# Where a transformer block sums its last softmax and its MLP's weight blocks

## The chip, the cores and the metric

The kernel runs on one core of a Trainium2 chip. The core has a matrix engine (TensorE, PE in the profile, with PEld for its weight loads), VectorE (DVE), ScalarE (ACT), GpSimd (POOL) and SyncE (SP), which issues most of the DMA transfers. Each engine works off its own queue in order and waits on semaphores for the others. TensorE reads SBUF and writes PSUM; the other engines take its results from there. The metric is the device time of one execution in microseconds (us), the median of several runs; lower is better.

## The reference, cut to what matters

A transformer block in fp32 on x of 16 x 224 x 512, with a context of 16 x 750 x 512 and 16 heads of 32: self-attention, cross-attention, and an MLP of hidden width 2048.

```python
x = x + gate_a[:, None] * attn_out            # self-attention, 224 keys
c_attn_w = softmax(einsum('bhqd,bhsd->bhqs', q_c, k_c) * scale, axis=-1)   # 750 keys
x = x + (c_attn_w @ v_c) @ W_cproj + b_cproj
x_norm2 = modulate(_ln(x), shift_m, scale_m)
h = gelu(x_norm2 @ W_mlp1 + b_mlp1)           # 512 -> 2048
x = x + gate_m[:, None] * (h @ W_mlp2 + b_mlp2)
```

## The kernel before

Every helper line is recorded in the profile as line 28 (the wrapper `Ordered` that keeps instructions in program order), so the profile is read by tile names. A product of two 4-byte operands shows as two records per matmul call.

**Cross-attention** runs over 64 units, a unit being one batch and a group of four heads. The 750 keys lie on partitions in six chunks of 125; three tiles `pt` of a unit hold two chunks each for four heads and 224 queries. The units are pipelined: while one unit's scores are made, the unit before it gets its maxima subtracted (`subtract`, VectorE) and its exponentials (`weights`, ScalarE), and the one before that is multiplied with the values (`values`, TensorE). `weights(h)` is called for the heads in two halves (h is 0 or 1). After each exponential GpSimd adds that tile's chunks onto `acc`: five additions of 125x448 for each half, ten for a unit. `values` then makes 24 matmuls of weights and values into a PSUM bank `o`, and `sums` four matmuls of ones and `acc`, which give the softmax denominators in the same bank. `finish` normalizes (`normalize`, VectorE: a reciprocal and a product) into `at`, which `project` multiplies with `wcproj`.

**The transition** (lines 1114 to 1145) runs after the last unit's maxima. TensorE's queue holds, in this order: the unit before the last (`prev.values`), the four plain products of MLP tile 0 (`mlp_plain`, into the four banks of `sc`) with the transposes of the two `subtract` calls between them, the last unit's `cur.values`, two products of MLP tile 1 (`ahead.begin`, banks `mm`), the two halves of the last projection (banks 0 and 1 of `tail`, tile name `sc`), and the other five products of tile 1 (`ahead.rest`). VectorE's queue holds `subtract`, `mlp_turned`, `mlp_sums(1)`, `cur.finish`, the addition in `begin`, the two `upd` of the projection, and the evictions of `rest`. The projection's x is finished on GpSimd and written to the DRAM tile `x_cross` by SP's queue; behind that write, in the same queue, are the loads of `w1_3` and of the four parts of `w2`, 1 MB each.

**The MLP** runs over 7 groups of 512 tokens (`GT`). Its products of 2 x 2 blocks use seven block products instead of eight: sums of blocks of both operands are made first (`combine` for the left one, `combine_right` for the right one; four operations each). For the first layer `mlp_sums(i)` makes the sums of weight tile i (i is 0 to 3, 512 of the 2048 columns): the tiles `ws` and a quarter of `w` itself; `mlp_turned` makes those of the tokens (`tt`, and a quarter of `mxt`). An operation of either has 128x512 elements. For the second layer `sums_2` makes those of `w2` in two rounds of four operations with 128x1024 elements, round 0 from `w2[0]` and `w2[2]`, round 1 from `w2[1]` and `w2[3]`.

`First(i)` is one weight tile for one group of tokens: `begin` makes products 1 and 2, `rest` products 6, 5, 7, 3 and 4 on the banks a, b and c, with an eviction between them (VectorE copies or adds; ScalarE copies and applies the gelu). Products 7 and 4 go on accumulating in bank a, so each waits until the bank's earlier content is read. In the first group (q = 0), tile 0 is plain, tile 1 is `ahead`, and then come `first(2)`, `mlp_sums(3)` on VectorE, `sums_2` on GpSimd, `first(3)`, and `mlp_sums(0)` on GpSimd (lines 1260 to 1264). `second(q, half)` is the second layer for half of a group's tokens: seven products of 16 records each, with operations on h by VectorE between them (`s1`, then `a21`, `a11`, `a12`), evictions into `upd`, and `close`, two GpSimd operations and the output's store. `between(p)` is called at fixed places in it and puts there the next group's loads, norms, transposes (`mlp_turn`) and `mlp_turned`.

Of the kernel before, what the change touches and what calls it, by code (L numbers as in the profile page):

```python
# [10 lines left out]
AF = mybir.ActivationFunctionType  # L11
ALU = mybir.AluOpType
# [25 lines left out]
def kernel(  # L38
# [23 lines left out]
    nc = Ordered(tc)  # L62
    B, N, H = x.shape
# [10 lines left out]
    CP = 125  # L74
# [12 lines left out]
    GC = GT // P  # L87
    HT = GT // 2
    NW = MLP // H
# [69 lines left out]
    def load_w(pool, w, name, bufs=1):  # L159
        kc = w.shape[0] // P  # L160
        t = pool.tile([P, kc, w.shape[1]], F32, name=name, bufs=bufs)
        nc.sync.dma_start(out=t, in_=w.rearrange("(k p) n -> p k n", p=P))
        return t
# [91 lines left out]
    for i in range(2):  # L255
        lo = (2 + 3 * i) * H
# [106 lines left out]
    def sums(o, pts, rows):  # L363

        for i, pt in enumerate(pts):
            for s in range(HG):
                mm(
                    o[s * HD : (s + 1) * HD, N : 2 * N], ones[:rows, :HD], pt[:, s, :],
                    start=False, stop=(i == len(pts) - 1), skip_group_check=True,
                )  # L370
# [36 lines left out]
    first = {}  # L407
# [28 lines left out]
    if True:  # L436
# [190 lines left out]
        for i, (p, g, j) in enumerate(units):  # L627
# [6 lines left out]
            if was:  # L634
                pt = self_weights(*was, row)
# [20 lines left out]
        pt = self_weights(*was, row)  # L656
# [18 lines left out]
    mlp = {"w1": [], "ws": {}, "w2": [], "wt": [], "h": {}}  # L675
# [10 lines left out]
    def mlp_weights(pool, name):  # L686
        i = len(mlp["w1"])
        mlp["w1"].append(load_w(pool, w_mlp1[:, i * H : (i + 1) * H], name))

    def combine(engine, a11, a12, a21, a22, s1, s2, s3, s4):  # L690

        engine.tensor_tensor(s1, a21, a22, ALU.add)
        engine.tensor_tensor(s3, a11, a21, ALU.subtract)
        engine.tensor_tensor(s2, s1, a11, ALU.subtract)
        engine.tensor_tensor(s4, a12, s2, ALU.subtract)

    def combine_right(engine, b11, b12, b21, b22, t1, t2, t3, t4):

        engine.tensor_tensor(t1, b12, b11, ALU.subtract)
        engine.tensor_tensor(t3, b22, b12, ALU.subtract)  # L700
        engine.tensor_tensor(t2, b22, t1, ALU.subtract)
        engine.tensor_tensor(t4, b21, t2, ALU.subtract)

    def mlp_sums(engine, pool, i):

        w = mlp["w1"][i]
        mlp["ws"][i] = ws = pool.tile([P, 3, 2, HT], F32, name=f"ws{i}", bufs=1)
        lo, hi = w[:, :2], w[:, 2:]
        combine(
            engine, lo[:, :, :HT], hi[:, :, :HT], lo[:, :, HT:], hi[:, :, HT:],  # L710
            ws[:, 0], ws[:, 1], lo[:, :, HT:], ws[:, 2],
        )

# [5 lines left out]
    def mlp_norm(i):  # L719
        Norm([mx[i]], [mx[i]], P).all()  # L720
# [18 lines left out]
                )  # L739
            lo = to  # L740

    def mlp_turned(engine):

        mlp["tt"] = tt = mlp["in"].tile([P, 3, 2, HT], F32, name="tt")
        lo, hi = mlp["xt"][:, :2], mlp["xt"][:, 2:]
        combine_right(
            engine, lo[:, :, :HT], lo[:, :, HT:], hi[:, :, :HT], hi[:, :, HT:],
            tt[:, 0], tt[:, 1], lo[:, :, HT:], tt[:, 2],
        )

    def mlp_plain(ps, m):

        w, lo = mlp["w1"][m // KC], (m % KC) * P
        for k in range(KC):
            mm(ps[:, :GT], w[:, k, lo : lo + P], mlp["xt"][:, k, :], start=(k == 0), stop=(k == KC - 1))
# [4 lines left out]
    class First:  # L760
# [39 lines left out]
            self.product(c, 2, True)  # L800
            nc.vector.tensor_tensor(self.p1, c, self.p1, ALU.add)

        def rest(self, b):
            a = self.a
            self.product(a, 6, False)
            u2 = self.part()
            nc.vector.tensor_copy(u2, a)
            self.product(b, 5, True)
            p5 = self.part()
            nc.scalar.copy(p5, b)  # L810
            self.out(self.p1, 0, 0)
            self.product(a, 7, False)
            nc.vector.tensor_tensor(p5, a, p5, ALU.add)
            self.out(p5, 1, 1)
            self.product(b, 3, False)
            nc.vector.tensor_tensor(u2, b, u2, ALU.add)
            self.out(u2, 0, 1)
            self.product(a, 4, False)
            self.out(a, 1, 0)


    wqc, wcproj, wkc, wvc = cw["qc"], cw["proj"], cw["k"], cw["v"]
    cxt_pool = context_pools.enter_context(tc.tile_pool(name="cxt", bufs=3, side="right", reuse_waits="tile"))
    with tc.tile_pool(name="ca", bufs=2, reuse_waits="tile") as ca:
# [98 lines left out]
        for b in range(B):  # L923
            n = b + 1
            for g in range(KC):
                f, m = (b, g + 1) if g < KC - 1 else (n, 0)
# [50 lines left out]
        class Unit:  # L977
# [72 lines left out]
                    w4 = pt[:, 2 * h : 2 * h + 2, :].rearrange("p s (k t) -> p s k t", k=2)  # L1050
                    nc.vector.tensor_tensor(w4, w4, less.to_broadcast([CP, 2, 2, N]), ALU.add)

            def weights(self, h):

                if h == 0:
                    self.acc = ca.tile([CP, HG, N], F32, name="acc", bufs=2)
                acc = self.acc[:, 2 * h : 2 * h + 2, :]
                for n, pt in enumerate(self.pts):
                    w = pt[:, 2 * h : 2 * h + 2, :]
                    nc.scalar.activation(w, w, AF.Exp)  # L1060

                    if n == 0:
                        nc.gpsimd.tensor_tensor(acc, w[:, :, :N], w[:, :, N:], ALU.add)
                    else:
                        for j in range(2):
                            nc.gpsimd.tensor_tensor(acc, acc, w[:, :, j * N : (j + 1) * N], ALU.add)

            def values(self):
                b, g = self.b, self.g
                self.o = ps_o.tile([P, 512], F32, name="o")  # L1070
                for n in range(CH):
                    values(
                        self.o, self.pts[n], lambda s, kc: vt[b, kc][:, (g * HG + s) * HD : (g * HG + s + 1) * HD],
                        (2 * n, 2 * n + 1), CP, n == 0,
                    )
                sums(self.o, [self.acc], CP)

            def finish(self):
                t = ca.tile([P, N], F32, name="at", bufs=2 * KC)
# [14 lines left out]
        cur = prev = last = None  # L1094
        for b, g in units:
            cur, prev, last = Unit(b, g), cur, prev
# [20 lines left out]
        prev.finish()  # L1117
        mlp_plain(sc[:, 1], 1)
        cur.subtract(0)
        cur.weights(0)  # L1120
        mlp_plain(sc[:, 2], 2)
        cur.subtract(1)
        cur.weights(1)
        mlp_plain(sc[:, 3], 3)
        mlp_turned(nc.vector)
        mlp_sums(nc.vector, mlp["in"], 1)
        for m in range(KC):
            gelu(sc[:, m], mlp["h"][0][:, m], m)
        cur.values()
        cur.finish()  # L1130
        ahead = First(1)
        ahead.begin(*(ps_mm.tile([P, 512], F32, name="mm") for _ in range(2)))
        tail = ps_s.tile([P, HG, 512], F32, name="sc")
# [5 lines left out]
    with tc.tile_pool(name="ml", bufs=3, reuse_waits="tile") as ml:  # L1139
# [1 line left out]
            mlp["h"][i] = ml.tile([P, KC, GT], F32, name=f"h{i}", bufs=1)  # L1141
        mlp_weights(ml, "w1_3")
        ahead.rest(tail[:, 2])
        mlp_sums(nc.vector, ml, 2)
        attention_psum.close()

        mlp["w2"] = [load_w(ml, w_mlp2[i * H : (i + 1) * H, :], f"w2_{i}") for i in range(NW)]
        bmlp2 = bias_rows(ml, b_mlp2, P, "bmlp2")
        resid = {}

        def sums_2():

            for i in range(NW // 2):
                t12 = (
                    cw["pool"].tile([P, KC, H], F32, name="wcproj") if i == 0
                    else ml.tile([P, KC, H], F32, name="w2t12", bufs=1)
                )
                t4 = ml.tile([P, KC, HT], F32, name=f"w2t4_{i}", bufs=1)
                lo, hi = mlp["w2"][i], mlp["w2"][i + NW // 2]
                combine_right(  # L1160
                    nc.gpsimd, lo[:, :, :HT], lo[:, :, HT:], hi[:, :, :HT], hi[:, :, HT:],
                    t12[:, :, :HT], t12[:, :, HT:], lo[:, :, HT:], t4,
                )
                mlp["wt"].append((t12[:, :, :HT], t12[:, :, HT:], t4))

        def fetch(i):
            t = ml.tile([P, H], F32, name="xr")
# [4 lines left out]
        with (  # L1172
# [3 lines left out]
            def bank(name):  # L1176
                return ps_p.tile([P, 512], F32, name=name)

            def first(i):
                f = First(i)  # L1180
                f.begin(bank("a"), bank("c"))
                f.rest(bank("b"))

            def second(q, half, between):

# [69 lines left out]
            for q in range(NG):  # L1255
                if q:
                    for i in range(NW):
                        first(i)
                else:
                    first(2)  # L1260
                    mlp_sums(nc.vector, ml, 3)
                    sums_2()
                    first(3)
                    mlp_sums(nc.gpsimd, ml, 0)

                def between(half, p, i=(q + 1) * GC, more=q + 1 < NG):

                    if not more:
                        return
                    if (half, p) == (0, 1):  # L1270
                        for c in range(GC):
                            mlp_load(i + c)
                    for c, at in enumerate(((0, 6), (0, 5), (0, 7), (0, 3))):
                        if (half, p) == at:
                            mlp_norm(i + c)
                    for c, at in enumerate(((0, 7), (0, 3), (1, 2), (1, 5))):
                        if (half, p) == at:
                            mlp_turn(ps_mm, i + c)
                    if (half, p) == (1, 5):
                        mlp_turned(nc.vector)  # L1280

                for half in range(2):
                    second(q, half, lambda p, half=half: between(half, p))
# [36 lines left out]
```

## Time and profile before

| | us |
|---|---|
| median of 3 runs (lowest to highest) | 2915.72 (2912.17 to 2917.97) |
| profiled execution | 2912.48 |
| span of its trace, first to last instruction | 2910.7 |

The mean granted TensorE clock in the profiled execution is 0.993 of full speed. Cut into stretches, the trace gives:

| stretch, us from the span's start | what runs | TensorE busy | VectorE | ScalarE | GpSimd | granted clock |
|---|---|---|---|---|---|---|
| 0 to 630 | mostly self-attention | 614.4 | 418.4 | 131.8 | 122.4 | 1.00 |
| 630 to 2189 | rest of it, cross-attention | 1514.6 | 1198.6 | 853.5 | 955.5 | 0.99 |
| 2189 to 2315 | the transition, first MLP group | 115.2 | 76.3 | 23.3 | 58.7 | 0.96 |
| 2315 to 2910.7 | the other six groups | 589.6 | 236.5 | 111.0 | 105.2 | 1.00 |

All edited code belongs to the third stretch, in which TensorE stands still for 10.9 of 126 us; in the last one it does so for 6.1 of 595.7. A row of the timeline has the start, the time from its first instruction's start to its last one's end, the engine, the operation with output and inputs, partitions x elements, a count, and in brackets the engine's idle time before it and what ended that.

### The profile page before, as it was taken

The page shows a single profiled execution, that of the slowest core. Times are in us where ns is not written, and L with a number is a line of the kernel's source. Part 1 is how long each engine was busy: PE and PEld are TensorE (multiplying, and loading weights), DVE is VectorE, ACT ScalarE, POOL GpSimd, SP SyncE. Part 2 cuts the span into 40 slices and gives each one's busy share as a digit, 9 for nine tenths or more (in the row PEclk, how much of TensorE's full clock was granted, in tenths as well). Part 3 has the DMA queues.
Part 4 walks back from the last instruction along what each step waited for, and adds up shares of the span by engine and source line. Part 5 has one row for each costly group of instructions (what it writes and reads, how often), then busy time and mean ns, then how long its engine had stood idle before and what let it go on. Part 6 is the DMA issues. An engine that isn't in the chain of part 4 may idle for free.

```text
span 2910.7 us, 46976 instructions
## 1 busy us (share of the span) xinstructions
PE 2833.8 (97%) x19693; PEld 1809.3 (62%) x19693; DVE 1929.8 (66%) x2752; ACT 1119.6 (38%) x1402; POOL 1241.7 (43%) x1379
## 2 busy tenths in 40 slices
PE   8999999998999999999999999999978999999999
PEld 3444444444555565655655655666545888888888
DVE  4666776676478778787787787787785543444343
ACT  1222222221456655665565556656543112112211
POOL 1022222122357666676666666666654410221021
PEclk9999999999999999999999999999989999999999
DMA  6111110100100010100001100100013111110110
GB/s 191 59 33 33 32 33 10 60 11 29 52 32 24 22 35 24 35 32 21 29 25 34 35 24 23 34 25 24 22 44 107 55 37 37 44 57 29 46 44 29
DMA packets 55385, 114.44 MB, mean 39 GB/s; under 512 B 4309, under 2 KB 4373, under 8 KB 55173
## 3 DMA queue, kind: packets, MB, share of 16 engines
q1 hardware_dynamic: 54560, 110.58, 11.8%
q8 instruction: 155, 2.54, 0.4%
q10 hardware_dynamic: 612, 0.85, 0.1%
q14 instruction: 58, 0.47, 0.1%
HBM read 89.33 MB, written 22.09 MB: 38 GB/s over the span
## 4 chain that ended last, share of the span: by engine, by line
PE 79%; DVE 10%; ACT 5%; issue 4%; POOL 2%; DMA 1%; SPq 0%; POOLq 0%; ACTq 0%; DVEq 0%
PE mm L28 43%; PE a L28 10%; PE sc L28 10%; PE o L28 8%; PE b L28 5%; ACT pt L28 4%; DVE at L28 3%; PE c L28 3%; DVE top L28 2%; POOL acc L28 1%; DVE stats L28 1%; DVE m L28 1%; DVE mc L28 1%; ACT kt L28 1%; DMA gate<-gate_d 1%
## 5 line engine op out<-in xcount | busy, mean ns | idle before, releaser
L28 POOL TENSOR_TENSOR acc<-acc,pt 125x448 f32<-125x448 f32 x512 | 584.4, 1141 | 40.2
L28 ACT COPY pt<-sc 125x1792 f32<-125x1792 f32 x192 | 317.3, 1653 | 563.0 <-DVE top L28 509.9
L28 DVE TENSOR_TENSOR pt<-pt,o 125x896 f32<-125x896 f32 x384 | 394.2, 1081 | 87.0 <-PE o L28 84.6
L28 DVE TENSOR_TENSOR top<-top,sc 125x896 f32<-125x896 f32 x320 | 346.6, 1083 | 35.4 <-PE sc L28 28.7
L28 PE MATMUL mm<-wkvc,cxt 128*125 128x512 f32 x768 | 354.4, 604 | 6.9 <-ACT kt L28 6.9
L28 PE MATMUL mm<-cxt,wkvc 128*128 128x375 f32 x1024 | 353.3, 487 | 2.4 <-ACT cxt L28 2.4
L28 POOL TENSOR_TENSOR upd<-upd,gate 112x512 f32<-112x512 f32 (+1 forms) x60 | 78.9, 1315 | 631.7 <-DVE upd L28 627.1
L28 ACT ACTIVATE pt<-pt 125x896 f32<-125x896 f32 x384 | 338.3, 951 | 18.7 <-DVE pt L28 18.1
L28 POOL TENSOR_TENSOR acc<-pt 125x448 f32<-125x448 f32 x128 | 146.6, 1145 | 455.6 <-ACT pt L28 455.6
L28 PEld LDWEIGHTS mm<-cxt,wkvc 128*128 128x128 f32 x1024 | 184.7, 190 | 118.9 <-issue 15.4
L28 PEld LDWEIGHTS mm<-wkvc,cxt 128*125 128x125 f32 x768 | 136.4, 187 | 171.5 <-issue 153.3
L28 DVE RECIPROCAL at<-o 128x224 f32<-128x224 f32 x128 | 198.7, 1552 | 66.9 <-PE o L28 66.9
L28 ACT ACTIVATE pt<-sc 112x1792 f32<-112x1792 f32 x64 | 106.5, 1664 | 332.5 <-PE sc L28 327.9
L28 POOL TENSOR_TENSOR rstd<-mv,eps 112x2 f32<-112x2 f32 (+3 forms) x93 | 18.0, 193 | 468.7 <-DVE mv L28 468.7
L28 PE MATMUL sc<-qt,kt 32*125 32x224 f32 x3072 | 201.5, 376 | 13.9 <-ACT pt L28 13.3
L28 PE MATMUL mm<-xt,wqkv 128*128 128x448 f32 x512 | 208.6, 550 | 5.7 <-DVE xt L28 4.7
L28 DVE TENSOR_REDUCE m<-sc 112x8 f32<-112x1792 f32 x64 | 129.6, 2025 | 121.0 <-PE sc L28 121.0
L28 PEld LDWEIGHTS sc<-qt,kt 32*125 32x125 f32 x3072 | 132.9, 183 | 93.7 <-issue 33.4
L28 PE MATMUL o<-pt,vt 125*32 125x224 f32 x3072 | 158.6, 354 | 0.0
L28 PEld LDWEIGHTS mm<-xt,wqkv 128*128 128x128 f32 x512 | 92.0, 190 | 87.6 <-issue 80.4
L28 DVE TENSOR_REDUCE mc<-mm 112x8 f32<-112x512 f32 (+1 forms) x128 | 79.8, 666 | 98.4 <-PE mm L28 98.3
L28 ACT COPY mx<-a 128x512 f32<-128x512 f32 x26 | 15.2, 585 | 325.4 <-POOL upd L28 306.3
(187 smaller groups left out, 4687.2 us busy)
## 6 DMA issues: line engine op xcount, KB each, us to landing
cx<-in_ctx_dram SPq DMA_DIRECT2D x96, 250.0 KB
x<-in_x_dram SPq DMA_DIRECT2D x16, 448.0 KB
x_self<-x SPq DMA_DIRECT2D x16, 448.0 KB
x<-x_self SPq DMA_DIRECT2D x16, 448.0 KB
x_cross<-x SPq DMA_DIRECT2D x16, 448.0 KB
mx<-x_cross SPq DMA_DIRECT2D x28, 256.0 KB
w<-in_L_xcond_W_mlp_dram SPq DMA_DIRECT2D x7, 1024.0 KB
xr<-x_cross SPq DMA_DIRECT2D x28, 256.0 KB
```

Of the source, the lines that this page charges most:

```text
L28: return lambda *args, **kw: self.tc.keep_in_program_order(f(*args, **kw))
```

## The change

- **The last unit's softmax sums.** `weights` gets a switch `add`. For the last unit it is off: the exponentials are taken as before, the GpSimd additions are left out, and `values` gives `sums` the six chunks instead of `acc`: 24 matmuls of ones and weights in place of four.
- **Order in the transition.** `mlp_turned` and `mlp_sums(1)` stand behind `cur.finish()`.
- **Block sums as generators.** `combine` and `combine_right` yield after each operation, so that a caller can issue them one at a time; `every` issues what is left. All of them are on VectorE now.
- **Tile 2.** `rest` calls `between` after each of its five eviction steps. `first(2)` issues one operation of `mlp_sums(3)` at each.
- **Tile 3.** `first(3)` issues two operations of `sums_2` at each, which were on GpSimd ahead of it.
- **`mlp_sums(0)`**, which was on GpSimd behind `first(3)`, is issued on VectorE at the place `between(3)` of the first half of `second(0, ...)`.
- **Load order.** The four `w2` parts are loaded as 0, 2, 1, 3.

```diff
+    def every(steps):
+        for _ in steps:
+            pass
     def combine(engine, a11, a12, a21, a22, s1, s2, s3, s4):
-        engine.tensor_tensor(s1, a21, a22, ALU.add)
+        yield engine.tensor_tensor(s1, a21, a22, ALU.add)
...
-        def rest(self, b):
+        def rest(self, b, between=lambda: None):
             self.product(a, 6, False)
             nc.vector.tensor_copy(u2, a)
+            between()
             self.product(b, 5, True)
             nc.scalar.copy(p5, b)
             self.out(self.p1, 0, 0)
+            between()
             self.product(a, 7, False)
             nc.vector.tensor_tensor(p5, a, p5, ALU.add)
             self.out(p5, 1, 1)
+            between()
             self.product(b, 3, False)
             nc.vector.tensor_tensor(u2, b, u2, ALU.add)
             self.out(u2, 0, 1)
+            between()
             self.product(a, 4, False)
             self.out(a, 1, 0)
+            between()
...
-            def weights(self, h):
+            def weights(self, h, add=True):
+                if not add:
+                    for pt in self.pts:
+                        w = pt[:, 2 * h : 2 * h + 2, :]
+                        nc.scalar.activation(w, w, AF.Exp)
+                    self.acc = None
+                    return
...
-                sums(self.o, [self.acc], CP)
+                if self.acc is None:
+                    sums(self.o, [pt[:, :, j * N : (j + 1) * N] for pt in self.pts for j in range(2)], CP)
+                else:
+                    sums(self.o, [self.acc], CP)
...
-        cur.weights(0)
+        cur.weights(0, False)
...
-        cur.weights(1)
+        cur.weights(1, False)
         mlp_plain(sc[:, 3], 3)
-        mlp_turned(nc.vector)
-        mlp_sums(nc.vector, mlp["in"], 1)
         for m in range(KC):
             gelu(sc[:, m], mlp["h"][0][:, m], m)
         cur.values()
         cur.finish()
+        mlp_turned()
+        every(mlp_sums(mlp["in"], 1))
...
-        mlp["w2"] = [load_w(ml, w_mlp2[i * H : (i + 1) * H, :], f"w2_{i}") for i in range(NW)]
+        w2 = {i: load_w(ml, w_mlp2[i * H : (i + 1) * H, :], f"w2_{i}") for i in (0, 2, 1, 3)}
+        mlp["w2"] = [w2[i] for i in range(NW)]
...
-                combine_right(
-                    nc.gpsimd, lo[:, :, :HT], lo[:, :, HT:], hi[:, :, :HT], hi[:, :, HT:],
+                yield from combine_right(
+                    nc.vector, lo[:, :, :HT], lo[:, :, HT:], hi[:, :, :HT], hi[:, :, HT:],
...
-                    first(2)
-                    mlp_sums(nc.vector, ml, 3)
-                    sums_2()
-                    first(3)
-                    mlp_sums(nc.gpsimd, ml, 0)
+                    steps = mlp_sums(ml, 3)
+                    first(2, lambda: next(steps, None))
+                    every(steps)
+                    steps = sums_2()
+                    first(3, lambda: (next(steps, None), next(steps, None)))
+                    every(steps)
...
+                    if (i, half, p) == (GC, 0, 3):
+                        every(mlp_sums(ml, 0))
```

More of the change, by code (lines that the diff above doesn't have):

```diff
@@ L688, in mlp_weights, with mlp_sums @@
         mlp["w1"].append(load_w(pool, w_mlp1[:, i * H : (i + 1) * H], name))
+    def every(steps):
+        for _ in steps:
+            pass
     def combine(engine, a11, a12, a21, a22, s1, s2, s3, s4):
-        engine.tensor_tensor(s1, a21, a22, ALU.add)
-        engine.tensor_tensor(s3, a11, a21, ALU.subtract)
-        engine.tensor_tensor(s2, s1, a11, ALU.subtract)
-        engine.tensor_tensor(s4, a12, s2, ALU.subtract)
+        yield engine.tensor_tensor(s1, a21, a22, ALU.add)
+        yield engine.tensor_tensor(s3, a11, a21, ALU.subtract)
+        yield engine.tensor_tensor(s2, s1, a11, ALU.subtract)
+        yield engine.tensor_tensor(s4, a12, s2, ALU.subtract)
     def combine_right(engine, b11, b12, b21, b22, t1, t2, t3, t4):
[L699 to L704, printed above, removed]
+        yield engine.tensor_tensor(t1, b12, b11, ALU.subtract)
+        yield engine.tensor_tensor(t3, b22, b12, ALU.subtract)
+        yield engine.tensor_tensor(t2, b22, t1, ALU.subtract)
+        yield engine.tensor_tensor(t4, b21, t2, ALU.subtract)
+    def mlp_sums(pool, i):
         w = mlp["w1"][i]
@@ L708, in mlp_sums @@
         lo, hi = w[:, :2], w[:, 2:]
-        combine(
-            engine, lo[:, :, :HT], hi[:, :, :HT], lo[:, :, HT:], hi[:, :, HT:],
+        return combine(
+            nc.vector, lo[:, :, :HT], hi[:, :, :HT], lo[:, :, HT:], hi[:, :, HT:],
             ws[:, 0], ws[:, 1], lo[:, :, HT:], ws[:, 2],
@@ L740, in mlp_turn, with mlp_turned @@
             lo = to
-    def mlp_turned(engine):
+    def mlp_turned():
         mlp["tt"] = tt = mlp["in"].tile([P, 3, 2, HT], F32, name="tt")
         lo, hi = mlp["xt"][:, :2], mlp["xt"][:, 2:]
-        combine_right(
-            engine, lo[:, :, :HT], lo[:, :, HT:], hi[:, :, :HT], hi[:, :, HT:],
+        every(combine_right(
+            nc.vector, lo[:, :, :HT], lo[:, :, HT:], hi[:, :, :HT], hi[:, :, HT:],
             tt[:, 0], tt[:, 1], lo[:, :, HT:], tt[:, 2],
-        )
+        ))
     def mlp_plain(ps, m):
@@ L1143 @@
         ahead.rest(tail[:, 2])
-        mlp_sums(nc.vector, ml, 2)
+        every(mlp_sums(ml, 2))
         attention_psum.close()
-        mlp["w2"] = [load_w(ml, w_mlp2[i * H : (i + 1) * H, :], f"w2_{i}") for i in range(NW)]
+        w2 = {i: load_w(ml, w_mlp2[i * H : (i + 1) * H, :], f"w2_{i}") for i in (0, 2, 1, 3)}
+        mlp["w2"] = [w2[i] for i in range(NW)]
         bmlp2 = bias_rows(ml, b_mlp2, P, "bmlp2")
@@ L1159, in sums_2 @@
                 lo, hi = mlp["w2"][i], mlp["w2"][i + NW // 2]
-                combine_right(
-                    nc.gpsimd, lo[:, :, :HT], lo[:, :, HT:], hi[:, :, :HT], hi[:, :, HT:],
+                mlp["wt"].append((t12[:, :, :HT], t12[:, :, HT:], t4))
+                yield from combine_right(
+                    nc.vector, lo[:, :, :HT], lo[:, :, HT:], hi[:, :, :HT], hi[:, :, HT:],
                     t12[:, :, :HT], t12[:, :, HT:], lo[:, :, HT:], t4,
                 )
-                mlp["wt"].append((t12[:, :, :HT], t12[:, :, HT:], t4))
         def fetch(i):
@@ L1177, in bank, with first @@
                 return ps_p.tile([P, 512], F32, name=name)
-            def first(i):
+            def first(i, between=lambda: None):
                 f = First(i)
                 f.begin(bank("a"), bank("c"))
-                f.rest(bank("b"))
+                f.rest(bank("b"), between)
             def second(q, half, between):
@@ L1279, in between @@
                     if (half, p) == (1, 5):
-                        mlp_turned(nc.vector)
+                        mlp_turned()
                 for half in range(2):
```

## The prediction, made before the changed kernel ran

> **What bounds the kernel now.** I read the first and fourth parts of the page, then TensorE's waits from 2180 to 2300 us, where all the edited code runs, then the timeline there.
>
> ```profile
> PE 2833.8 (97%) x19693; PEld 1809.3 (62%) x19693; DVE 1929.8 (66%) x2752; ACT 1119.6 (38%) x1402; POOL 1241.7 (43%) x1379
> ...
> PE 79%; DVE 10%; ACT 5%; issue 4%; POOL 2%; DMA 1%; SPq 0%; POOLq 0%; ACTq 0%; DVEq 0%
> ```
> TensorE (PE) is busy 97% of the span and holds 79% of the chain that ended last. The change can win only gaps of TensorE and lose only by making new ones or adding matmuls. The waits name the gaps (total, times, longest, in us):
>
> ```profile
> PE o L28 <- POOL acc L28: 6.2, 1, 6.2
> PE a L28 <- DVE ws L28: 3.8, 1, 3.8
> ...
> PE sc L28 <- DVE upd L28: 0.8, 1, 0.8
> ```
> The first is the softmax sum of the last cross-attention unit, waiting for GpSimd (POOL); the second is tile 3 of the MLP's first layer, waiting for its block sums on VectorE (DVE). In the timeline (start, duration, engine, operation, idle before):
>
> ```profile
> 2204.18 2.48 PE L28 MATMUL o<-pt,vt 125*32 125x224 f32 x48
> ...
> 2207.16 6.05 POOL L28 TENSOR_TENSOR acc<-acc,pt 125x448 f32<-125x448 f32 x4
> ...
> 2213.27 0.96 PE L28 MATMUL o<-acc,ones 125*32 125x224 f32 x4 [6.24 <-POOL acc L28]
> ...
> 2223.53 3.69 PE L28 MATMUL sc<-wcproj,at 128*112 128x512 f32 x8 [0.78 <-DVE upd L28]
> ...
> 2234.77 0.68 DVE L28 TENSOR_TENSOR ws<-wqc 128x512 f32<-128x512 f32 x1
> ...
> 2249.55 2.77 DVE L28 TENSOR_TENSOR w<-w 128x512 f32<-128x512 f32 x1
> ...
> 2255.22 3.37 PE L28 MATMUL a<-tt,ws 128*128 128x256 f32 x8 [3.83 <-DVE ws L28]
> ```
> The same VectorE operation takes 0.68 us at 2234.77 and 2.77 at 2249.55: beside the second, GpSimd runs `sums_2` (128x1024, 2.4 to 2.8 us each), and the engines alternate one for one. Each long gap also costs clock afterwards. The windows of 1 us (length, busy time and count of PE, PEld, DVE, ACT, POOL, then the granted clock) show it:
>
> ```profile
> 2171.00:2172.00 1.00, 0.00 (x0) 0.00 (x0) 1.00 (x2) 0.30 (x1) 0.00 (x0) 1.00 0.00 0
> ...
> 2173.00:2174.00 1.00, 0.60 (x8) 0.57 (x12) 1.00 (x2) 1.00 (x2) 0.00 (x0) 0.50 0.00 0
> ...
> 2215.00:2216.00 1.00, 1.00 (x3) 0.76 (x3) 0.97 (x2) 0.00 (x0) 0.00 (x0) 0.50 0.00 0
> ...
> 2256.00:2257.00 1.00, 1.00 (x3) 0.79 (x3) 1.00 (x1) 0.00 (x0) 1.00 (x1) 0.50 0.00 0
> ```
> After both gaps the clock is 0.50; eight matmuls take 3.37 instead of 1.73 us (row at 2255.22).
>
> **A. The last unit's sums.** Removed: its ten GpSimd additions, the gap and the slow clock after it. Before, from the first value product (2204.18) to the first product of `ahead.rest` (2227.22 in the chain) is 23.04 us. After, on TensorE:
> - values and sums: `sums` gets six pieces instead of one, 24 matmuls, 48 records where there were 8. They have the values' shape, whose chain piece is 56 records in 2.79 us, 0.050 each: 96 x 0.050 = 4.8, to 2208.96. The 40 added records are 2.0 us on the path. The last exponentials end at 2204.91, before their products come up, so no wait takes the old one's place.
> - products 1 and 2 of `ahead.begin` at full clock: 2 x 1.73 = 3.45, to 2212.4. They read none of the quarters that the sums rewrite (at 2249.50 such a product ran beside such a rewrite).
> - first half of the last projection: 3.45, to 2215.9.
> - `mlp_turned` and `mlp_sums(1)` are moved behind `cur.finish()` in VectorE's queue. VectorE idles from 2203.9; reciprocal and product (1.55 + 0.39 + issue) run from 2209.15 to 2211.1, the eight moved operations, now without GpSimd, take 8 x 0.69 = 5.5, to 2216.6; queued behind them are the addition of `begin` (0.70) and the first `upd` (0.69), to 2218.05. The second half of the projection waits for that `upd`, as in the row at 2223.53. What is late next is VectorE: this wait grows from 0.8 to 2.2 us.
> - second half 3.69: rest begins at 2221.75. **Gain of A: 5.47 us.**
>
> The final additions to x on GpSimd, the x_cross write behind them and the weight loads behind that in SP's queue follow the second projection and come earlier too. Before, the loads issue from 2229.89, and GpSimd finds its last needed one at 2246.6.
>
> **B. Tiles 2 and 3.** Before, `first(2)` takes 7 x 1.73 = 12.1 us, `first(3)` 12.1 + 3.83 + 1.64 of slow clock. Undone: 5.47. Added to VectorE:
> - In `first(2)`, four steps of 0.69, one after each of four evictions (0.69). 1.4 us against a product's 1.73: hidden. They need w1_3, now about 12 us after the loads begin. Before, GpSimd found the third load behind w1_3 landed 16.7 us after the first issue, at about 3 us a load ((2246.6 - 2240.5) / 2), which puts w1_3 at 7.7: some 4 us to spare. Without that cover the queue would hold the evictions and the gap would show at once.
> - In `first(3)`, eight operations of 128x1024 in pairs. The trace has none on VectorE. The lower bound is twice 0.69 less one start; the upper, 2.4 to 2.8, GpSimd's duration for it and VectorE's beside GpSimd. Nearest is VectorE's own addition of 112x896, 1.13: scaled by the 0.45 between 512 and 896 elements, 1.22, with issue 1.24. GpSimd is now idle here, so I take 1.24.
> - From product 6's start: copy u2 ends at 2.62, four steps at 7.58, the p5 addition at 8.29. Product 4 overwrites that bank: 8.33 instead of 6.90, **1.43 us lost**. Two steps, u2's addition and two steps end at 13.96. Behind them in `second` four operations on h (2.80), an eviction (0.34), the first a11 (0.70): 17.8. TensorE, after product 4 (10.06) and two of 3.45, is free at 16.96: **0.88 lost**. ACT's last gelu ends near 13.3, just before the second of those products (13.5).
> - The load order (0, 2, 1, 3) brings the pair 0 and 2 in first; with about 3 us a load and tile 3's steps some 12 us after tile 2's, no step waits.
>
> **Gain of B: 5.47 - 2.31 = 3.16 us.**
>
> **C. `mlp_sums(0)`** leaves GpSimd (four of 1.6 to 1.7 us at 2264.75, hidden) for VectorE, between the last two products of the first half:
>
> ```profile
> 2286.74 0.42 DVE L28 TENSOR_TENSOR upd<-b,upd 128x256 f32<-128x256 f32 x1 [1.40 <-PE b L28]
> ...
> 2287.25 1.27 POOL L28 TENSOR_TENSOR upd<-upd,gate 128x512 f32<-128x512 f32 x1 [1.03 <-DVE upd L28]
> ...
> 2290.63 0.42 DVE L28 TENSOR_TENSOR upd<-a,bmlp 128x256 f32<-128x256 f32 x1 [0.66 <-PE a L28]
> ...
> 2292.75 1.75 DVE L28 TENSOR_TENSOR s<-h,h 128x512 f32<-128x512 f32 x1
> ...
> 2296.44 1.28 DVE L28 TENSOR_TENSOR h<-s,h 128x512 f32<-128x512 f32 x2
> ...
> 2297.77 1.89 PE L28 MATMUL a<-wcproj,h 128*128 128x256 f32 x8
> ```
> They start right after the row at 2286.74. Queued behind are a norm's statistics (0.9), eight modulations (2.1), the eviction at 2290.63, four operations on h, an eviction and a11 at 2296.44, for which the product at 2297.77 waits; a11's first half is ready at 2297.08, 0.85 before TensorE is free (2297.93 in the chain). Upper bound: beside GpSimd's two gate operations (2287.25) two of the four last 1.65, as at 2292.75; all four end 4.68 after they start. Less VectorE's idle 0.66 and the 0.85, and 0.45 because the norm no longer meets the operations on h (5.13 now, 2 x 0.69 + 2 x 1.65 then): 2.72. Lower bound, nothing shared: 2.8 - 0.66 - 0.85 = 1.3. GpSimd's operations stand there in the trace, so I take the upper. **Loss of C: 2.72 us.**
>
> **Sum.** 5.47 + 3.16 - 2.72 = 5.9 us, from span 2910.7 to 2904.8. The profiled execution took 2912.48, so 2906.6 for one like it. The median of the three runs is 3.24 above that execution; carried onto it the gain gives **2909.8**, or 0.20%.
>
> **The clock speaks against part of this.** The new gaps are 2.2 (A), 1.4 and 0.9 (B) and 2.7 us (C). The Trainium skill, TensorE: Matmul & The Clock Gate (Why this matters for your kernels), asks only for no idle gap over some 3 us; by that none costs clock and the sum stays 5.9. The trace is stricter: a gap of 2.69 us at 2170.7, with one of 1.23 just before it, led to 0.50 (rows above), while 0.78 at 2222.8 cost nothing. The page (Part 1) also says that the gate judges in fixed windows of about 3.4 us, so the phase decides. By the row both larger gaps cost a slow window, each up to the 1.7 us seen: the sum is 2.5. I take the sum without them, since either gap may be split over two windows, and keep 2.5 for a rival and the range.
>
> **Rivals.**
> - *C is hidden* (25%). If `mlp_sums(0)` takes the lower price or its delay is absorbed, 7.3 to 8.6 us are gained: 2908.4 to **2907.1**. For: the delay must pass a slack and an idle stretch; against: both are counted.
> - *The new gaps cost clock* (20%). 2.5 gained: **2913.2**, no change that can be told. For: the row at 2173; against: B's gaps are short.
> - *VectorE becomes tile 3's bound, slower than before* (13%). With d for a 1024-wide step the two losses of B sum to 8d - 7.6 (2.3 at 1.24). The gain is 15.8 - 8d: zero at d = 1.98, and a loss that can be told from d = 2.7. At 2.5 the gaps are 6.4 and 6 us and bring two slow windows of 1.7: 4.2 + 3.4 = 7.6 lost, **2923.3**. For: VectorE's rows of 2.7 in this very stretch; against: GpSimd is gone from it, and at 2235 the operations took 0.69 with the DMA engines full.
>
> The forecast itself has 42%. About 0.2% (5.8 us) is what a measurement of this kernel can tell from no change; my sum sits on that line. Of the forecast 24 points fall to faster and 18 to same; with the first rival's 25, the second's 18 same and 2 slower, the third's 10 slower and 3 same: 0.49 faster, 0.39 same, 0.12 slower. The range runs from 2904.5 (C hidden and TensorE not waiting for `upd`, 8.6 + 2.2 = 10.8) to 2917 (both slow windows, and d near 1.7, where 3.7 more is lost).
>
> **What would show it.** A: no GpSimd acc after 2198; 48 records o<-pt,ones; the wait of sc on upd near 2.2 us. B: no wait of a on ws; VectorE's 128x1024 rows near 1.22; a wait of a on mx near 1.4. C: four ws/w operations of VectorE after the first half's b, partly near 1.65, and a wait of a on h near 2.7. The prediction is wrong if steps wait for a DMA, if d is near 2, or if the clock column shows 0.50 after the small gaps.

## The result, and the profile after

| | before | changed |
|---|---|---|
| median of 13 runs each, us (lowest to highest) | 2915.36 (2912.10 to 2918.32) | 2909.49 (2905.12 to 2911.71) |
| profiled execution, us | 2912.48 | 2907.90 |
| span of its trace, us | 2910.7 | 2906.1 |
| mean granted clock | 0.993 | 0.993 |

The ratio is 0.9979, with a 95% interval of 0.9972 to 0.9986: 5.9 us faster by the medians, and 4.6 in the two profiled executions. Both gaps that the prediction wanted to close are closed, and the three new waits that it named are there. TensorE's waits of the changed kernel from 2195 to 2320 us (total, times, longest):

```profile
PE a L28 <- DVE h L28: 2.7, 1, 2.7
PE sc L28 <- DVE upd L28: 1.5, 1, 1.5
PE a L28 <- DVE mx L28: 1.0, 1, 1.0
```
The waits for GpSimd's acc (6.2) and for ws (3.8) are gone; those for h (place C) and for mx (tile 3, place B) are new; the one for upd (place A) has grown from 0.8. The rows of the changed kernel's timeline behind them (start, duration, engine, operation, idle before):

```profile
2208.75 2.45 PE L28 MATMUL o<-pt,ones 125*32 125x224 f32 x48
...
2219.82 3.69 PE L28 MATMUL sc<-wcproj,at 128*112 128x512 f32 x8 [1.53 <-DVE upd L28]
...
2238.68 0.69 DVE L28 TENSOR_TENSOR w<-w 128x512 f32<-128x512 f32 x1
...
2250.05 1.21 DVE L28 TENSOR_TENSOR wcproj<-w 128x1024 f32<-128x1024 f32 x1
...
2251.30 1.23 DVE L28 TENSOR_TENSOR w<-w,w 128x1024 f32<-128x1024 f32 x1
...
2252.44 1.22 DVE L28 TENSOR_TENSOR wcproj<-w,wcproj 128x1024 f32<-128x1024 f32 x1
...
2255.57 1.99 PE L28 MATMUL a<-tt,w 128*128 128x256 f32 x8 [0.99 <-DVE mx L28]
...
2279.67 1.64 POOL L28 TENSOR_TENSOR upd<-upd,gate 128x512 f32<-128x512 f32 x1 [1.03 <-DVE upd L28]
2280.22 1.64 DVE L28 TENSOR_TENSOR w<-w 128x512 f32<-128x512 f32 x1
...
2281.78 1.75 DVE L28 TENSOR_TENSOR ws<-ws,w 128x512 f32<-128x512 f32 x1
...
2293.06 1.99 PE L28 MATMUL a<-wcproj,h 128*128 128x256 f32 x8 [2.70 <-DVE h L28]
```
Read from top to bottom: the 48 records of ones take 2.45 us right behind the values; the second half of the projection waits 1.53; a step of tile 2 takes 0.69 where it took 2.77; a 1024-wide step takes 1.21 to 1.23; product 4 of tile 3 is 0.99 late; the second of tile 0's block sums meets the gate multiplication, and both take 1.64, the third takes 1.75; the product for which the operations on h are needed is 2.70 late.

For everything that follows I cut the edited stretch at instructions that every version has: **S1** from the last unit's first value product to the first product of `ahead.rest`, **S2** from there to the first product of `second(0, 0)`, **S3** to the first transpose in it, **S4** to the first product of the next group.

| kernel (what differs from the changed one) | entry, us | S1 | S2 | S3 | S4 | sum | median, us (runs) | ratio to before, 95% |
|---|---|---|---|---|---|---|---|---|
| before | 2204.18 | 22.88 | 38.27 | 17.31 | 32.84 | 111.30 | 2915.36 (13) | |
| changed | 2206.46 | 16.88 | 34.07 | 17.66 | 35.80 | 104.41 | 2909.49 (13) | 0.9979 (0.9972 to 0.9986) |
| e1 (only A) | 2205.85 | 16.89 | 39.45 | 17.27 | 32.83 | 106.44 | 2911.21 (11) | 0.9987 (0.9978 to 0.9996) |
| e2 (without A) | 2204.68 | 23.01 | 34.07 | 17.66 | 35.81 | 110.55 | 2914.79 (11) | 0.9999 (0.9990 to 1.0008) |
| e3 (tile 0 on GpSimd) | 2204.21 | 16.89 | 34.06 | 17.67 | 32.83 | 101.45 | 2904.16 (5) | 0.9961 (0.9949 to 0.9974) |
| e4 (order back) | 2209.34 | 16.14 | 34.06 | 17.67 | 35.81 | 103.68 | 2910.01 (1) | |
| e5 (w2 sums on GpSimd) | 2207.64 | 16.89 | 32.80 | 17.27 | 37.49 | 104.45 | 2909.14 (1) | |
| e6 (longer gap) | 2208.09 | 16.88 | 34.07 | 17.66 | 39.37 | 107.98 | 2913.09 (1) | |
| e7 (no new waits) | 2204.14 | 16.14 | 32.80 | 17.27 | 32.83 | 99.04 | 2902.46 (5) | 0.9955 (0.9942 to 0.9967) |
| e8 (e7, own bank) | 2208.26 | 15.11 | 32.80 | 17.27 | 32.84 | 98.02 | 2902.63 (5) | 0.9956 (0.9942 to 0.9969) |
| e9 (tile 0 earlier) | 2208.00 | 16.89 | 34.07 | 17.66 | 32.84 | 101.46 | 2906.46 (1) | |

"Entry" is the time of the first value product from the start of the trace. All kernels run the same instructions up to there, and still it lies between 2204.14 and 2209.34. The ratio is to runs of the kernel before that were made beside each kernel's own, so it is not the quotient of two medians in this table (beside e1, e2 and e3 the median of before was 2915.10, beside e7 and e8 2916.70). The stages come from one trace of each kernel; they repeat to 0.13 us where nothing in them was changed and the clock fell alike. So the stages carry the explanation, and the medians only confirm it. Between before and changed the stages give 6.00 (S1), 4.20 (S2), -0.35 (S3) and -2.96 (S4), 6.89 in all; the profiled execution of the changed kernel entered 2.28 later, which leaves the 4.6 of its span. From S4's end to the last instruction both take 595.2 us.

### The profile page after: what moved, and what is told of

The parts are those of the page before. It is cut to its first block, busy times and chain, and to the rows that moved or that the text cites. A ratio compares the mean times of both kernels' runs of the same rounds, so it can differ in the third digit from the quotient of the medians.

```text
span 2906.1 us, 47040 instructions
## 1 busy us (share of the span) xinstructions
PE 2834.6 (98%) x19733; PEld 1810.3 (62%) x19733; DVE 1926.2 (66%) x2764; ACT 1119.7 (39%) x1402; POOL 1201.5 (41%) x1357
## 5 line engine op out<-in xcount | busy, mean ns | idle before, releaser
L28 POOL TENSOR_TENSOR acc<-acc,pt 125x448 f32<-125x448 f32 x504 | 573.6, 1138 | 39.5
```

Source lines behind the costliest of these rows:

```text
L28: return lambda *args, **kw: self.tc.keep_in_program_order(f(*args, **kw))
```

## The experiments

**e1, part A alone.** The last unit's sums and the order of the transition as in the changed kernel, the rest as before:

```diff
-                    steps = mlp_sums(ml, 3)
-                    first(2, lambda: next(steps, None))
-                    every(steps)
-                    steps = sums_2()
-                    first(3, lambda: (next(steps, None), next(steps, None)))
-                    every(steps)
+                    first(2)
+                    every(mlp_sums(ml, 3))
+                    every(sums_2())          # on nc.gpsimd again
+                    first(3)
+                    every(mlp_sums(ml, 0, nc.gpsimd))
-                    if (i, half, p) == (GC, 0, 3):
-                        every(mlp_sums(ml, 0))
```

> Only part A of the change (last unit's sums on TensorE, block sums behind finish); tiles 2 and 3, mlp_sums(0) and the load order as before. Stages measured from the trace: S1 first value product of the last unit to the first product of ahead.rest, S2 from there to the first product of second(0,0), S3 to the first transpose in it, S4 to the first product of the next group (before: 22.88, 38.27, 17.31, 32.84; changed: 16.88, 34.07, 17.66, 35.80). Theory (three independent parts, A -6.0, B -3.9, C +3.0): S1 16.9, S2 38.3 with the wait of a on ws near 3.8, S3 17.3, S4 32.8; median about 2909.4, no worse than the changed kernel. Rival (the parts do not add, because the gain is one of clock windows): S1 17 but a slow window elsewhere, median nearer 2912.

S1, S3 and S4 came as the theory had them. S2 did not quite: its wait of a on ws is 3.6 us, but the stage took 39.45, 1.18 more than before. Without any wait S2 takes 32.80 (e7), so the gap of 3.83 us cost 5.47 in the trace of before, 1.64 beyond its length, and the gap of 3.61 cost 6.65 here, 3.04 beyond it. The windows behind the two gaps, e1 first and then before (length, busy time and count of PE, PEld, DVE, ACT, POOL, then granted clock, share and GB/s of DMA), show why:

```profile
2249.53:2252.94 3.41, 2.26 (x5) 1.85 (x6) 3.38 (x2) 0.00 (x0) 3.33 (x3) 0.50 0.02 5
2252.94:2256.35 3.41, 3.41 (x9) 2.70 (x8) 1.64 (x3) 0.00 (x0) 3.41 (x2) 0.50 0.00 0
```
```profile
2254.65:2258.07 3.42, 2.85 (x7) 2.34 (x8) 3.38 (x3) 0.00 (x0) 3.34 (x2) 0.50 0.00 0
2258.07:2261.48 3.41, 3.41 (x18) 3.00 (x17) 1.05 (x2) 1.07 (x3) 3.41 (x2) 1.00 0.00 0
```
The clock was at half for 6.8 us in e1 and for 3.4 in before, so matmuls ran at half speed for 5.67 and for 2.85 us. Half of the difference is 1.41, and 1.40 was measured. So the rival's slow clock is there, as a longer stay after a gap that before has too; the other stages add as the theory said. The median, 2911.21, lies between the two expectations.

**e2, everything but part A.**

```diff
-        cur.weights(0, False)
+        cur.weights(0)
-        cur.weights(1, False)
+        cur.weights(1)
         mlp_plain(sc[:, 3], 3)
+        mlp_turned()
+        every(mlp_sums(mlp["in"], 1))
...
-        mlp_turned()
-        every(mlp_sums(mlp["in"], 1))
```

> The changed kernel with part A undone (GpSimd adds the last unit's weights again, block sums before the gelus). Theory: S1 22.9 with the 6.2 us wait of o on acc, S2 34.1, S3 17.7, S4 35.8; about 0.9 us under the kernel before, median about 2914.5. Rival (the spread steps are what made the gain): median near 2910.

As the theory had it, stage by stage. Tiles 2 and 3 gain 3.85 us, and the place of `mlp_sums(0)` takes 2.97 of it back. Over the four stages 0.75 us is left, too little for the medians: the interval of the ratio includes 1. Two of TensorE's waits in e2, the old one beside the new one:

```profile
PE o L28 <- POOL acc L28: 6.2, 1, 6.2
PE a L28 <- DVE h L28: 2.7, 1, 2.7
```

**e3, the block sums of tile 0 back on GpSimd.**

```diff
                     every(steps)
+                    every(mlp_sums(ml, 0, nc.gpsimd))
...
-                    if (i, half, p) == (GC, 0, 3):
-                        every(mlp_sums(ml, 0))
```

> The changed kernel with mlp_sums(0) given back to GpSimd, behind tile 3. Theory: GpSimd is idle since the last x, so the four operations run some 15 to 35 us before anyone needs GpSimd, S4 returns to 32.8, no wait of a on h; 3.0 us under the changed kernel, median about 2906.5. Rival (they meet the steps of tiles 2 and 3 on VectorE and are paid there): S2 or S3 grows by 2 to 4 us and the median stays at 2909.5.

S4 is back at 32.83 and S2 and S3 are unchanged, so the rival is out: nothing is paid elsewhere. All that TensorE still waits for from 2195 to 2320 us:

```profile
PE sc L28 <- DVE upd L28: 1.5, 1, 1.5
PE a L28 <- DVE mx L28: 1.0, 1, 1.0
```
The median fell by more than the stage (5.3 us below the changed kernel's, where the stage gives 2.97). With five runs and entries that differ by 5 us the medians cannot carry that difference.

**e4, the old order in the transition**, the sums still on TensorE: the two calls moved as in e2, the `weights` calls as in the changed kernel.

> The changed kernel with mlp_turned and mlp_sums(1) back ahead of the gelus in program order, the sums still on TensorE. VectorE idles 5.1 us there and needs 5.4 for the eight operations. Theory: they run from the end of subtract, the reciprocal starts up to 0.4 us later, the wait of sc on upd falls from 1.53 to about 0.8, S1 16.1 to 16.3. Rival (the move is needed, since the reciprocal is late by more than the projection can wait): S1 at 17 or above.

S1 fell by 0.74 to 16.14, and the wait for upd is 0.8. So part A did not need the move: once GpSimd's additions are gone, all but some 0.2 us of the eight operations fits into VectorE's idle time ahead of the reciprocal, which starts 5.04 us after the entry here and 4.81 in the changed kernel.

**e5, the sums of w2 on GpSimd, in the new places.**

```diff
-                    nc.vector, lo[:, :, :HT], lo[:, :, HT:], hi[:, :, :HT], hi[:, :, HT:],
+                    nc.gpsimd, lo[:, :, :HT], lo[:, :, HT:], hi[:, :, :HT], hi[:, :, HT:],
```

> The changed kernel with sums_2 on GpSimd, issued in the same places of the program. GpSimd runs it as soon as the weights land, beside tile 2's steps on VectorE. Theory (GpSimd's two-input operations hold up VectorE's two-input operations from SBUF one for one, and not its evictions from PSUM): the last of the ws/w steps of 128x512 in tile 2 take 2.4 to 2.8 instead of 0.69 us, GpSimd's 128x1024 up to 2.8 instead of 2.4, tile 2 gets a wait of a on mx of 1 to 3 us, tile 3 none; S2 between 34 and 36. Rival (the transfers into SBUF slowed VectorE before, not GpSimd): the steps stay at 0.69, no wait in either tile, S2 33.1.

Rows of VectorE and of GpSimd in the timeline of e5:

```profile
2242.67 2.25 DVE L28 TENSOR_TENSOR ws<-ws,w 128x512 f32<-128x512 f32 x1
2244.85 0.68 DVE L28 TENSOR_TENSOR mx<-b,mx 128x512 f32<-128x512 f32 x1
2245.45 2.28 DVE L28 TENSOR_TENSOR ws<-w,ws 128x512 f32<-128x512 f32 x1
```
```profile
2242.01 2.37 POOL L28 TENSOR_TENSOR w<-w,w 128x1024 f32<-128x1024 f32 x1 [1.49 <-DMA w<-in_L_xcond_W_mlp_dram]
2244.32 2.86 POOL L28 TENSOR_TENSOR wcproj<-w,wcproj 128x1024 f32<-128x1024 f32 x1
2247.26 2.68 POOL L28 TENSOR_TENSOR w2t<-w,wcproj 128x1024 f32<-128x1024 f32 x1
```
The cause of the slow rows is GpSimd, as the theory said: the steps at 2242.67 and 2245.45 end some 0.55 us after GpSimd's operation beside them has ended (2244.92 against 2244.38, 2247.73 against 2247.18), as if they had stood still until then, while the addition at 2244.85, one of whose inputs is in PSUM, keeps its 0.68 in the middle of such an operation. The size of the harm was a miss: three slow steps of 1.9 to 2.3 fit between the evictions, no wait arose in tile 2, and S2 came to 32.80, less than with VectorE doing it all. So, with the rest as in the changed kernel, spreading the steps of tile 2 is enough. What cost 3.8 us before was that all four stood in a block ahead of tile 3, each held up by GpSimd. (No run spreads them in the kernel before and changes nothing else.)

e5 also has an S4 of 37.49, with the same wait of 2.7 us on h. One-microsecond windows of e5 (length, busy time and count of PE, PEld, DVE, ACT, POOL, then granted clock, share and GB/s of DMA) and below them those of the changed kernel, each from its gap on, show what differs:

```profile
2291.00:2292.00 1.00, 0.00 (x0) 0.00 (x0) 1.00 (x3) 0.00 (x0) 0.00 (x0) 1.00 0.81 283
...
2294.00:2295.00 1.00, 1.00 (x4) 0.74 (x4) 1.00 (x4) 0.00 (x0) 0.00 (x0) 0.50 0.62 219
...
2296.00:2297.00 1.00, 1.00 (x4) 0.82 (x3) 0.00 (x0) 0.00 (x0) 0.00 (x0) 0.50 0.18 41
```
```profile
2292.00:2293.00 1.00, 0.00 (x0) 0.00 (x0) 1.00 (x4) 0.00 (x0) 0.00 (x0) 1.00 0.81 246
...
2294.00:2295.00 1.00, 1.00 (x6) 0.87 (x6) 1.00 (x2) 0.00 (x0) 0.00 (x0) 1.00 0.81 244
...
2296.00:2297.00 1.00, 1.00 (x6) 0.90 (x5) 0.60 (x3) 0.00 (x0) 0.00 (x0) 1.00 0.45 135
```
The same gap of 2.7 us is followed by half the clock in e5 (four matmuls in a microsecond instead of six or seven) and not in the changed kernel. The clock records of the traces show what decides. In each of the eleven traces the granted clock changes only at points that lie whole multiples of 3.41 us apart, which divide the trace into stretches of that length. Here are the stretches that hold most of the gap, and the one after them, first of e5, then of the changed kernel:

```profile
2290.48:2293.89 3.41, 1.29 (x6) 1.16 (x7) 3.38 (x7) 0.00 (x0) 0.00 (x0) 1.00 0.67 209
2293.89:2297.30 3.41, 3.41 (x10) 2.70 (x9) 2.07 (x6) 0.00 (x0) 0.00 (x0) 0.50 0.52 175
```
```profile
2288.13:2291.55 3.42, 2.23 (x13) 1.74 (x11) 3.38 (x3) 0.00 (x0) 2.59 (x2) 1.00 0.00 0
2291.55:2294.96 3.41, 1.90 (x9) 1.70 (x10) 3.41 (x7) 0.00 (x0) 0.00 (x0) 1.00 0.80 262
2294.96:2298.37 3.41, 3.41 (x18) 3.00 (x17) 1.88 (x6) 0.00 (x0) 0.00 (x0) 1.00 0.37 125
```
In e5 one stretch takes 2.12 us of the gap, and TensorE is busy for 38% of it; in the changed kernel the gap is split over two, which stay 65% and 56% busy. In e2 and e4, which kept their clock too, the emptier stretch is 51% and 52% busy. From 650 us on, over all eleven traces, every full-clock stretch in which TensorE was busy for less than 46% was followed by half the clock, and none above 53% was.

**e6, a longer gap at the same place.**

```diff
                         every(mlp_sums(ml, 0))
+                        ws, w0 = mlp["ws"][0], mlp["w1"][0]
+                        for _ in range(3):
+                            nc.vector.tensor_tensor(ws[:, 2], w0[:, 2:, :HT], w0[:, :2, HT:], ALU.subtract)
```

> The changed kernel with the last operation of mlp_sums(0) issued three times more (the same values written again): 3 x 0.70 = 2.1 us more on VectorE there, so that the wait of a on h grows from 2.7 to 4.8 us. Theory (a gap of 2.7 stays free of clock loss, one well over 3.4 us costs a slow window): S4 35.8 + 2.1 = 37.9 and up to 1.7 more, with granted clock 0.50 in rows after the gap. Rival (the clock after the gaps of before fell for another reason than their length): S4 37.9, clock 1.00.

The repeated operation subtracts the rewritten quarter of w, not `ws[:, 1]`, so it changes the third block sum of tile 0, which product 3 of that tile uses from the second group on; its engine, size and place are those expected. The wait and the clock behind it in e6:

```profile
PE a L28 <- DVE h L28: 4.9, 1, 4.9
```
```profile
2297.00:2298.00 1.00, 1.00 (x3) 0.82 (x4) 1.00 (x3) 0.00 (x0) 0.00 (x0) 0.50 0.78 260
```
S4 is 39.37, 3.57 more than in the changed kernel: 2.17 by the longer gap, and 1.40 for the slow clock. The gap leaves the whole stretch from 2292.92 to 2296.33 idle, and the clock falls at its end. So a longer gap at this place does cost clock, as the theory had it; that a gap of 2.7 stays free does not hold (e5).

**e7, all three new waits taken away.** `mlp_sums(0)` on GpSimd as in e3, the order of e4, and three steps of `sums_2` ahead of tile 3:

```diff
                     steps = sums_2()
-                    first(3, lambda: (next(steps, None), next(steps, None)))
+                    for _ in range(3):
+                        next(steps)
+                    first(3, lambda: next(steps, None))
                     every(steps)
+                    every(mlp_sums(ml, 0, nc.gpsimd))
```

> The changed kernel with all three new waits taken away: mlp_sums(0) on GpSimd, mlp_turned and mlp_sums(1) ahead of the gelus, three of the eight steps of sums_2 issued on VectorE ahead of tile 3 and one at each of its five places. Theory: S1 16.1, S2 33.1 (no wait of a on mx), S3 17.3, S4 32.8, sum 99.4 against 104.4 of the changed kernel and 111.3 of before; median about 2904.4 (5.0 under the changed kernel's 2909.5). Rival (the three early steps wait for the load of w2_2 or hold up the addition of tile 3's begin): a wait for DMA on VectorE, S2 at 34 or above.

One wait is left from 2195 to 2320 us:

```profile
PE sc L28 <- DVE upd L28: 0.8, 1, 0.8
```
S2 is 32.80, which is nineteen products of 1.727: no gap at all. At 99.04 the stages are 5.37 below the changed kernel's, and the ratio to before is 0.9955 (0.9942 to 0.9967). The median, 2902.46, is 7.0 below the changed kernel's, again more than the stages give.

**e8, a bank of its own for the projection's second half.** e7, and:

```diff
-            project(B - 1, c, tail[:, c])
+            project(B - 1, c, tail[:, c] if c == 0 else ps_mm.tile([P, 512], F32, name="mm"))
```

> As the one before, and the second half of the last projection goes into a bank of its own (mm) instead of bank 1 of the tile that holds the first half. Theory (the wait of the second half on the first half's upd comes from both halves lying in one tile, though in different banks): the wait of sc on upd is gone, S1 falls by another 0.7 to 0.8 to 15.4, sum 98.6, median about 2903.7. Rival (the second half has to wait for VectorE for another reason): S1 stays at 16.1.

The trace of e8 shows no wait of TensorE in the stretch, and S1 is 15.11, 1.03 below e7's: the wait of 0.78, and 0.25 that the forecast of 15.4 did not count. So the 0.8 us of before came from both halves lying in one tile. The sum is 98.02; the median, 2902.63, cannot be told from e7's.

**e9, `mlp_sums(0)` on VectorE, three products earlier.**

```diff
-                    if (i, half, p) == (GC, 0, 3):
+                    if (i, half, p) == (GC, 0, 6):
```

> The changed kernel with mlp_sums(0) left on VectorE but issued three products earlier in the same half, at between(6) instead of between(3). GpSimd has nothing with two inputs there and VectorE idles 2.2 us behind each eviction. Theory (the wait of a on h came from the place: GpSimd's gate operations double two of the four operations, and the chain behind them has only 0.85 us to spare): the four ws/w operations take 0.69 each, no wait of a on h, S4 32.8. Rival (VectorE has too much to do in this half, wherever the 2.8 us are put): S3 and S4 together stay near 53.5.

Two of the four rows in e9:

```profile
2270.26 0.68 DVE L28 TENSOR_TENSOR ws<-w 128x512 f32<-128x512 f32 x1
2270.97 0.69 DVE L28 TENSOR_TENSOR w<-w 128x512 f32<-128x512 f32 x1
```
S3 and S4 together are 50.50, no wait on h is left. The loss of C came from the place, not from the work: VectorE has room for the 2.8 us three products earlier.

## Why the prediction was right

The forecast was 2909.8 us, a gain of 5.9; the median is 2909.49, a gain of 5.87. The parts show how much of that agreement is earned.

- **A, forecast 5.47, measured 6.00 (S1).** The mechanism is the predicted one: the path goes over to VectorE's queue, and the second half of the projection waits for upd. That wait was put at 2.2 us and is 1.53. The terms that were too large are the eight operations (5.5 forecast; 5.31 from 2213.17 to the next start at 2218.48) and the value and sum products (4.8; 4.68 from 2206.46 to the next product at 2211.14); the other 0.2 lies in the smaller steps of VectorE's queue. What the prediction left out is that the move which made this wait was not needed (e4).
- **B, forecast 3.16, measured 3.85 (4.20 in S2, less 0.35 in S3).** The first loss, 1.43 forecast, is a wait of 0.99 and 1.27 in S2 (34.07 against 32.80); the second, 0.88 forecast, is 0.39 in S3 (17.66 against 17.27). The duration scaled from the 896-wide row, 1.22, was right to 0.01. The term that was too large is the start-to-start time: 1.24 was taken for every step, but starts are 1.25 and 1.14 apart in turn. The 1.14 stands where a step does not need the one just before it (the second overwrites what the first reads, the third uses only the first's result, the fourth the third's), and begins before that one has ended.
- **C, forecast 2.72, measured 2.96 (S4, of which the wait is 2.70).** The choice of the upper bound was right: two of tile 0's four operations take 1.64 and 1.75 beside GpSimd's gate operations. The prediction put both at 1.65, though the row it names, at 2292.75, has 1.75. e9 shows that this came from the place.
- **The clock.** The sum was made without a slow window for the new gaps, against a row that showed one after 2.69 us. In the changed kernel's trace no new gap lost clock, nor did the 2.7 us in e2 and e4; in e5 the same gap cost 1.69. So the 2.7 us gap lost clock in one trace of four. The prediction's reason, that the gap may be split over two windows, is what the traces show (e5). That the split fell so in the changed kernel's trace is luck: the trace of before cannot tell where the windows of another execution will lie. How many of the 13 runs lost clock there is not shown. The Trainium skill (TensorE: Matmul & The Clock Gate, Why this matters for your kernels) puts the limit at some 3 us; e5 shows that 2.7 can be enough.
- **The rivals.** C was not hidden. Tile 3 was not bound by VectorE beyond the two small losses: a step took 1.22, far from 1.98. Steps waited for no transfer; the loads were issued from 2226.17 instead of 2229.89. The new load order was not tried by itself.

The three misses, +0.53, +0.69 and -0.24, add to 0.98 in the stages. That the medians agree to 0.3 us is luck: their own scatter is larger than that. One slip in the prediction's sums changes nothing here: the lower end of its range should be 2904.9 by its own 10.8, not 2904.5.

## What to carry to other kernels

When work is moved between engines, follow the queue it is moved into up to the next instruction that the bound engine needs: every loss of this change was a short chain in VectorE's queue, and another place in the same queue took each away, or back to its old size in the case of A, without giving back the gain (e4, e7, e9). In this kernel VectorE needed no relief from GpSimd where its work was spread between evictions (e5), and much where it stood as a block ahead of a product. A gap on TensorE does not have one price: the gap of 2.7 us cost 2.96 in the changed kernel's S4 and 4.65 in e5's, by where it lay between the changes of the clock. For effects of a few us in 2900, cut the trace at instructions that both versions have and compare the stages.

## What the runs showed that was not expected

Up to the first edited instruction all eleven kernels run the same instructions, yet they reach the entry between 2204.14 and 2209.34 us. Part of the spread arises early, where self-attention ends and TensorE has gaps: between 696 and 718 us the clock is at 0.50 for 10 to 20 us, depending on the execution. The value products that start at 2070.92 in the trace of before start at 2071.95 in the changed kernel's and at 2075.06 in e4's, with the same instructions ahead of them. That is about the scatter of the 13 runs (2912.10 to 2918.32 before), so a good part of it is likely the clock's answer to the same gaps. The clock records support this: up to the entry TensorE was busy at half clock for 26 to 35 us. Half of that time is lost, and over the eleven traces the entry comes 0.99 us later for each us lost (a straight line through the eleven points, correlation 0.96). No run changed the clock by itself.
